# Segment maxima over neighbour windows in 640-column turned tiles, in a graph-attention kernel on one core

## The chip, the cores and the metric

The kernel runs on one core of one Trainium2 chip. A core has five engines that run side by side, each with its own stream of instructions: TensorE (PE; its weight loads are listed as PEld), VectorE (DVE), ScalarE (ACT), GpSimd (POOL) and SyncE (SP, which here only issues transfers), and 16 DMA engines that move data. The metric is the device time of one execution in microseconds (us).

## The reference

A graph has 3125 nodes with a vector x of 128 values each, and 100000 edges (src, dst, type), sorted by dst; the type is one of 5 relations. With 8 heads of 16 values, for each relation r:

```python
mask = edge_types == r
q, k, v = x_dst @ W_Q[r], x_src @ W_K[r], x_src @ W_V[r]     # per head
logits = (q * k).sum(-1) / scale + attn_bias[r]
masked = where(mask, logits, NEG)
max_v  = segment_max(masked, dst)
exp_l  = where(mask, exp(masked - max_v[dst]), 0)
attn   = exp_l / (segment_sum(exp_l, dst)[dst] + 1e-12)
out   += segment_sum(attn * v, dst)
```

Then `h = layernorm(out @ out_proj.T + b + x) * gamma + beta`, and the result is `layernorm(x + h)`. What matters below: a softmax needs the largest logit among all the edges of one node, one relation and one head, and the edges of a node lie next to each other.

## The kernel before

**Tiling.** The edges are cut into 196 groups of 512 (GE). A step k handles three groups; the last two of the 66 steps handle two. In a group, 128 edges stand on the partitions and T = 4 tiles follow each other. A lane is one (group, relation, head): 3 x 5 x 8 = 120 lanes a step, and a lane tile has the lanes on the partitions and the 512 edges of the group along its columns.

**Preamble.** x is loaded and transposed; a table of keys and values for each node and relation is written to DRAM (kv_d), the node number of each edge as key rows (key_d), the masks that mark where a new node begins (msk_d), and queries (q_d), each query in three bf16 parts so that their sum is exact enough.

**One step.** The work of an edge group goes through these functions:

- `gather` (L603): POOL issues 12 indirect transfers, each of which fetches 128 rows of kv_d into one of six K/V buffers. `gather(k+3)` stands in step k and must wait until `weigh(k-3)` has read that buffer.
- `fetch`: SP issues the keys kt (L661, 384 KB, one row spread over 128 partitions, two buffers), the query rows qw (L668, three transfers with an offset read from a register) and the masks mk (L671, three transfers, each spread over 40 lanes) of step k+3.
- `spot` (L679, DVE) compares kt with the row number into a one-hot matrix, `spread_q` (L692, PE) multiplies it with qw: 36 small products in a step give each edge its query (qe).
- `products` (L706, DVE: K times qe), `logits` (L711 sums over each head, L713 adds a hugely negative number for the relations that an edge is not in), `turn_logits` (L725, PE: four transposes to 120 lanes x 512 columns), `keep_logits` (L734, ACT: a copy).
- `scans` (L741 and L744, DVE): a running maximum forwards and one backwards along the lane, each restarted by the mask where a new node begins. The result is each edge's segment maximum within its group.
- `joins` (L760 to L763, SP): a node can reach across the end of a group. Four transfers of 120 to 320 bytes copy the last or first maximum of a lane to the neighbouring lane's partition (tile c), two of them between this step and the one before.
- `less_max`: two DVE instructions (L770) put the neighbours' maxima into the first and the last 64 columns (SEG), where the mask shows that the node goes on; a third (L774) subtracts the maximum. `exps` (L781, ACT) takes the exponential.
- `turn_exps` (L788, PE) turns the exponentials back and drops the relation axis, `weights` (L797, ACT) copies them beside the weighted values, `weigh` (L803, DVE) multiplies them with V. It is the last reader of the K/V buffer.
- `places` (L811, L814, ACT) builds a matrix that says which row of a node window each edge belongs to, `sums` (L831, L827, PE) adds the weighted values up by it, `norm` (L843 to L847, DVE) divides by the sums, `relations` (L860, PE) and `by_node` (L865, ACT) add the relations and put the nodes in place.

Two pieces of work for each block of 128 nodes come in beside this. New queries of a block are computed over three steps: `turn_q` and `turned` in the step given by a table, then `queries`, `first_part` (ACT), `remainder` (DVE), `second_part` (ACT) and `third_part` (DVE) for three relations in the next step and for two in the one after, which ends with `store_q` (L652, SP). And when all edges of a block are done, `project`, `residual` (L890, L892), `roots` and `norms` (L907) finish its nodes; x comes for both in separate transfers (`fetch_x`, tiles xq and xr, L614).

**Order.** Nothing reorders the instructions: each engine runs its own in the order of the program, and semaphores hold them until their inputs are there. The steps overlap by hand. In step k the order is: gather(k+3), queries, less_max and exps of k-2, turn_exps and weights of k-2, products, logits and turn_logits of k, keep_logits, norm of k-3, the last part of the queries and `store_q`, weigh(k-2), sums, scans(k), joins(k), `take(k)` (all of SP's loads), spot(k+2), and the block's last work. On SP this means store_q, the four joins, then kt, qw, mk and x.

Of the kernel before, what the change touches and what calls it, by code (L numbers as in the profile page):

```python
# [17 lines left out]
P = 128  # L18
N = 3125
# [36 lines left out]
MW = GE + 1 + 2 * SEG  # L56
# [67 lines left out]
def windowed_path(  # L124
# [21 lines left out]
    shut = keep("shut", [P, NST, T * G3, R], BF16)  # L146
# [25 lines left out]
    xn = load.tile([P, NT, H], F32, name="xn")  # L172
# [39 lines left out]
    dst_r = load_rows("dst_r", dst, FAR)  # L212
# [7 lines left out]
    near = load.tile([HG, 2, 2], I32, name="near")  # L220
    nc.vector.memset(near, -1)
    ends = dst[: (NGR - 1) * GE].rearrange("(g i) -> g i", i=GE)
    with nc.allow_non_contiguous_dma(reason="one element of each group"):
        nc.gpsimd.dma_start(
            lr[:, : NGR - 1],
            dst[: (NGR - 1) * GE].rearrange("(o g i) -> o g i", o=1, i=GE)[:, :, GE - 1],
        )
        nc.gpsimd.dma_start(lr[:, NGR - 1 :], dst[E - 1 : E].rearrange("(o g) -> o g", o=1))
        nc.gpsimd.dma_start(near[1:HG, 0, 0:1], ends[: HG - 1, GE - 1 : GE])
        nc.gpsimd.dma_start(near[:HR, 1, 0:1], ends[HG - 1 :, GE - 1 : GE])  # L230
        nc.gpsimd.dma_start(near[:HG, 0, 1:2], ends[1 : HG + 1, 0:1])
        nc.gpsimd.dma_start(near[: HR - 2, 1, 1:2], ends[HG + 1 :, 0:1])
        nc.gpsimd.dma_start(
            near[HR - 2 : HR - 1, 1, 1:2],
            dst[(NGR - 1) * GE : (NGR - 1) * GE + 1].rearrange("(o g) -> o g", o=1),
        )
# [3 lines left out]
    def iota(name, pattern, n, base=0, mult=0, dt=F32, pool=const):  # L240
# [21 lines left out]
    nc.vector.tensor_scalar(rsum, five, 0.0, None, op0=ALU.is_le)  # L262
    nc.vector.scalar_tensor_tensor(
        rsum, five, -float(R), rsum, op0=ALU.is_gt, op1=ALU.mult
    )
# [77 lines left out]
    def lanes():  # L343
        nc.vector.tensor_scalar(lane, lane, 0.0, None, op0=ALU.is_equal)
# [57 lines left out]
    def masks_a():  # L402
        nc.vector.memset(msk[:, :, 0:1], -BIG)
        nc.vector.memset(msk[:, :, GE : GE + 1], -BIG)
        nc.vector.tensor_tensor(
            msk[:, :, 1:GE], dst_r[:, :, 1:], dst_r[:, :, : GE - 1], op=ALU.not_equal
        )
        nc.vector.tensor_scalar_mul(msk[:, :, 1:GE], msk[:, :, 1:GE], -BIG)

    def masks_b():  # L410
        nearf = load.tile([HG, 2, 2], F32, name="nearf")
        nc.vector.tensor_copy(nearf, near)
        for s in range(2):
            for n, c in enumerate((0, GE - SEG)):
                m = GE + 1 + n * SEG
                nc.vector.tensor_scalar(
                    msk[:, s, m : m + SEG], dst_r[:, s, c : c + SEG], nearf[:, s, n : n + 1],
                    -BIG, op0=ALU.not_equal, op1=ALU.mult,
                )
# [21 lines left out]
    def put_typ(ep, s, r):  # L441
        done, g0, n = 0, s * HG, HR if s else HG
        while done < n:
# [4 lines left out]
                shut[:, k0 : k0 + m, : T * i, r].rearrange("p k (t i) -> p k t i", i=i),  # L448
# [160 lines left out]
    def fetch_x(name, b):  # L609
        n = min(P, N - b * P)  # L610
        xb = flow.tile([P, H], F32, name=name, bufs=2 if name == "xq" else 4)
        if n < P:
            nc.vector.memset(xb, 0.0)
        nc.sync.dma_start(xb[:n], x[b * P : b * P + n, :])  # L614
        live[name, b] = xb

    def turn_q(b):
        tp = ps.tile([P, P], F32, name="tp", tag="fin")
        nc.tensor.transpose(tp, live.pop(("xq", b)), ident)
# [37 lines left out]
    def fetch(k):  # L657
# [11 lines left out]
        mk = flow.tile([L3, MW], BF16, name="mk", bufs=5)  # L669
        for i, g in enumerate(gs):  # L670
            nc.sync.dma_start(  # L671
                mk[i * LANES : (i + 1) * LANES, :], msk_d[g].partition_broadcast(LANES)
            )
        live["kt", k], live["qw", k], live["mk", k] = kt, qw, mk
# [33 lines left out]
    def logits(k):  # L708
        n = T * len(groups(k))
        lg = ps.tile([P, T * G3, HEADS], F32, name="lg")[:, :n]  # L710
        nc.vector.tensor_reduce(lg, heads(live.pop(("prod", k))[:, :n]), AX.X, ALU.add)  # L711
        lx = flow.tile([P, T * G3, R, HEADS], F32, name="lx")
        nc.vector.tensor_tensor(  # L713
            lx[:, :n],
            lg[:, :, None, :].to_broadcast([P, n, R, HEADS]),
            shut[:, k, :n, :, None].to_broadcast([P, n, R, HEADS]),
            op=ALU.add,
        )
        live["lx", k] = lx

    def turn_logits(k):
        n, lx = len(groups(k)), live.pop(("lx", k))
        lt = ps.tile([L3, GE], F32, name="lt")
        for t in range(T):
            nc.tensor.transpose(  # L725
                lt[: n * LANES, t * P : (t + 1) * P],
                lx[:, t * n : (t + 1) * n].rearrange("p g r k -> p (g r k)"), ident,
            )
        live["lt", k] = lt

    def keep_logits(k):
        n = len(groups(k)) * LANES
        ls = flow.tile([L3, GE], F32, name="ls", bufs=3)
        nc.scalar.copy(ls[:n], live["lt", k][:n])  # L734
        live["ls", k] = ls

    def scans(k):
        n = len(groups(k)) * LANES
        mk, lt = live["mk", k], live.pop(("lt", k))
        m = flow.tile([L3, GE], F32, name="m", bufs=3)  # L740
        nc.vector.tensor_tensor_scan(  # L741
            lt[:n], mk[:n, :GE], lt[:n], -BIG, op0=ALU.add, op1=ALU.max
        )
        nc.vector.tensor_tensor_scan(  # L744
            m[:n, ::-1], mk[:n, GE:0:-1], lt[:n, ::-1], -BIG, op0=ALU.add, op1=ALU.max
        )
        live["m", k] = m

    def joins(k):
        n = len(groups(k)) * LANES  # L750
# [874 lines left out]
```

## Time and profile before

| what | us |
|---|---|
| median of 3 runs (lowest to highest) | 1532.03 (1531.99 to 1539.9) |
| the profiled execution | 1544.54 |
| its span, first to last instruction | 1542.7 |
| mean granted clock of TensorE | 0.694 of full speed |
| gathers: 782 instructions of POOL | 750.4 busy, 960 ns each |
| PE idle ahead of the weight loads of L692 | 333.4 |
| POOL idle ahead of the gathers | 683.6 |
| L741 scan, 120x512 | 1.22 |
| L803 weigh | 1.73 |

The profile was taken of one execution. Its page gives each engine's busy time, the chain of work that ended last, the costliest groups of instructions, and the transfers. A group's row reads: line, engine, operation, output <- inputs, count, busy time, mean ns of one, then the idle time of the engine just before these instructions and what ended most of it. A row of the waits reads: who waited <- for whom: us in total, how many times, the longest. A row of the timeline reads: start, length, engine, line, operation, and in brackets how long the engine was idle before and what released it. "issue" means that the profile shows nothing that the engine waited for; "remote" means a releaser that the trace does not hold. SPq are SP's transfers as it issues them.

### The profile page before, as it was taken

What the parts mean: (1) busy time and instruction counts of PE and PEld (TensorE: products, weight loads), DVE (VectorE), ACT (ScalarE), POOL (GpSimd) and SP (SyncE); (2) the same over time, 40 slices, a digit from 0 to 9 for tenths busy, and PEclk for the clock granted to TensorE, in tenths of its full rate; (3) what the DMA queues carried; (4) which work ended last, traced back from release to release, by engine and by line L of the source; (5) the groups of instructions that cost most, each with busy time, mean ns of one, the idle gap of its engine ahead of it and who ended that gap; (6) DMA issues with size and microseconds to landing.
All of it is one profiled execution on the core that took longest, in us unless ns stands there. A gap on an engine that the chain in (4) does not pass through costs nothing.

```text
span 1542.7 us, 18732 instructions
## 1 busy us (share of the span) xinstructions
PE 996.5 (65%) x5955; PEld 767.6 (50%) x5955; DVE 873.6 (57%) x1363; ACT 617.2 (40%) x1635; POOL 762.6 (49%) x854
## 2 busy tenths in 40 slices
PE   6930166666666656467776666767777766666875
PEld 3510154555544545356555555555555555555664
DVE  4750264656554655366665656566656665555872
ACT  2420033444434434244444444444444444444662
POOL 3067433555563563635555555555555555555300
PEclk9955567666676776676766676666666667777876
DMA  6754243444442453434444444444444444444300
GB/s 210 286 181 146 71 130 92 131 128 121 142 136 83 141 148 92 134 92 142 129 119 124 141 135 122 144 143 120 140 132 124 122 139 135 126 140 129 93 18 8
DMA packets 126821, 196.27 MB, mean 127 GB/s; under 512 B 40507, under 2 KB 86200, under 8 KB 126593
## 3 DMA queue, kind: packets, MB, share of 16 engines
q0 software_dynamic: 37856, 102.55, 22.9%
q1 hardware_dynamic: 87724, 91.13, 18.8%
q10 hardware_dynamic: 1132, 1.31, 0.3%
q8 instruction: 49, 0.80, 0.2%
q14 instruction: 60, 0.48, 0.1%
HBM read 164.43 MB, written 30.40 MB: 126 GB/s over the span
## 4 chain that ended last, share of the span: by engine, by line
PE 28%; issue 21%; another core or an unknown queue 18%; DVE 16%; ACT 7%; DMA 1%; SPq 0%; DVEq 0%; ACTq 0%
PE both L831 10%; PE qe L692 7%; DVE wv L803 3%; PE nodes L860 3%; ACT at L811 3%; PE lt L725 3%; DVE lt L741 2%; PE both L827 2%; PE ex L788 2%; DVE prod L706 2%; DVE lg L711 2%; ACT ls L781 1%; DVE m L744 1%; DVE hot L679 1%
## 5 line engine op out<-in xcount | busy, mean ns | idle before, releaser
L603 POOL DMA_INDIRECT kv<-kv_d,idx x782 | 750.4, 960 | 683.6 <-DVE wv L803 395.9
L692 PE MATMUL qe<-qw,hot 125*128 125x128 bf16 x2352 | 250.4, 262 | 311.5 <-issue 243.4
L831 PE MATMUL both<-wv,at 128*125 128x136 f32 x1568 | 370.2, 384 | 20.0 <-ACT oT L865 7.5
L692 PEld LDWEIGHTS <-hot 125*128 125x128 bf16 x2352 | 203.4, 122 | 333.4 <-issue 326.5
L831 PEld LDWEIGHTS both<-wv,at 128*125 128x125 f32 x1568 | 295.8, 263 | 96.1 <-issue 74.4
L811 ACT ACTIVATE at<-row_at,nkey 128x125 f32<-128x125 f32 x784 | 247.3, 389 | 0.1
L706 DVE TENSOR_TENSOR prod<-kv,qe 128x1536 f32<-128x1536 f32 (+1 forms) x66 | 114.2, 1731 | 55.3 <-remote 55.3
L803 DVE TENSOR_TENSOR wv<-kv,ex 128x1536 f32<-128x1536 f32 (+1 forms) x66 | 114.2, 1730 | 36.4 <-ACT wv L797 36.4
L741 DVE TENSOR_TENSOR_SCAN lt<-mk,lt 120x512 f32<-120x512 bf16 (+1 forms) x66 | 80.6, 1222 | 87.8 <-ACT ls L734 87.8
L814 ACT ACTIVATE at<-at 128x500 f32<-128x500 f32 x196 | 121.6, 620 | 6.2
L725 PE MATMUL lt<-ident,lx 128*120 128x128 f32 (+1 forms) x264 | 73.4, 397 | 77.7 <-issue 70.4
L734 ACT COPY ls<-lt 120x512 f32<-120x512 f32 (+1 forms) x66 | 38.8, 587 | 206.5 <-PE lt L725 116.6
L711 DVE TENSOR_REDUCE lg<-prod 128x96 f32<-128x1536 f32 (+1 forms) x66 | 115.1, 1745 | 2.3
L860 PE MATMUL nodes<-rsum,o 125*128 125x25 f32 x392 | 87.7, 359 | 41.8 <-issue 30.1
L860 PEld LDWEIGHTS nodes<-rsum,o 125*128 125x128 f32 x392 | 85.5, 307 | 48.0 <-issue 33.6
L788 PE MATMUL ex<-gather_heads,ls 120*128 120x24 f32 (+1 forms) x528 | 71.9, 275 | 52.7 <-ACT ls L781 30.1
L788 PEld LDWEIGHTS ex<-gather_heads,ls 120*128 120x128 f32 (+1 forms) x528 | 68.8, 200 | 72.7 <-ACT ls L781 40.7
L639 DVE TENSOR_TENSOR prq<-prq,q 128x384 f32<-128x384 f32 (+1 forms) x42 | 20.9, 497 | 146.6 <-ACT q L635 120.8
L827 PE MATMUL both<-wv,over 128*5 128x136 f32 x390 | 97.1, 340 | 0.0
L725 PEld LDWEIGHTS lt<-ident,lx 128*120 128x120 f32 (+1 forms) x264 | 45.0, 196 | 104.0 <-issue 93.6
L797 ACT COPY wv<-ex 128x96 f32<-128x96 f32 (+1 forms) x66 | 15.8, 239 | 191.2 <-remote 182.2
L635 ACT CAST q<-prq 128x384 bf16<-128x384 f32 (+1 forms) x42 | 17.7, 422 | 184.2 <-remote 172.9
(157 smaller groups left out, 940.7 us busy)
## 6 DMA issues: line engine op xcount, KB each, us to landing
kt<-key_d SPq DMA_DIRECT2D x64, 384.0 KB
qw<-q_d SPq DMA_DIRECT2D x196, 96.0 KB
kv_d<-kvs SPq DMA_DIRECT2D x24, 640.0 KB
kv<-kv_d,idx POOLq DMA_INDIRECT x782
q_d<-q SPq DMA_DIRECT2D x25, 480.0 KB
mk<-msk_d SPq DMA_DIRECT2D x196, 50.1 KB
c<-m SPq DMA_DIRECT2D x134, 0.2 KB
c<-m SPq DMA_DIRECT2D x128, 0.3 KB
```

The lines of the kernel that those rows point to most:

```text
L603: nc.gpsimd.indirect_dma_start(out=kv[:, t * n + i, :], out_offset=None, in_=kv_d[:, :], in_offset=bass.IndirectOffsetOnAxis(ap=idx[:, t, ...
L692: nc.tensor.matmul(qe[:, t * n + i, :], hot[:, i, t * P : (t + 1) * P], qw[:WR, i, s, :], start=(s == 0), stop=(s == 2),)
L706: nc.vector.tensor_tensor(prod[:, :n], kv[:, :n, :H], qe[:, :n], op=ALU.mult)
L711: nc.vector.tensor_reduce(lg, heads(live.pop(("prod", k))[:, :n]), AX.X, ALU.add)
L725: nc.tensor.transpose(lt[: n * LANES, t * P : (t + 1) * P], lx[:, t * n : (t + 1) * n].rearrange("p g r k -> p (g r k)"), ident,)
L788: nc.tensor.matmul(ex[:, t * n : (t + 1) * n], ls[: n * LANES, t * P : (t + 1) * P], gather_heads[: n * LANES, :n], start=True, stop=True,)
L803: nc.vector.tensor_tensor(heads(wv[:, :n, :H]), heads(kv[:, :n, H:]), ex[:, :, :, None].to_broadcast([P, n, HEADS, HD]), op=ALU.mult,)
L811: nc.scalar.activation(at[:, t, :], row_at[:, :WR], AF.Abs, bias=nkey[:, t, g : g + 1], scale=1.0)
L814: nc.scalar.activation(at, at, AF.Relu, bias=1.0, scale=-1.0)
L827: nc.tensor.matmul(pp[:R], over[:, g, :], live["wv", last][:, t * len(groups(last)) + j, :], start=False, stop=False,)
L831: nc.tensor.matmul(pp[:WR], at[:, t, :], wv[:, t * n + i, :], start=(t == 0), stop=(t == T - 1))
L860: nc.tensor.matmul(nodes[:, i], o5[:, i], rsum[:WR], start=True, stop=True)
```

## The change

1. **Windows instead of joins.** A lane now sees 64 logits of the group before and 64 of the group behind, so the scans run over 640 columns and find each maximum without its neighbours' help. The logits tile gets room for one more group per tile of edges. `near` (DVE, 64 x 40) writes the first 64 edges of this step's first group into the tile of the step before; `pass_on` (ACT, 64 x 40) copies the last 64 edges of the step into the next step's tile. Turning takes two more transposes of 64 edges: one in `turn_logits`, one in `turn_next`. The scans work in place in PSUM, over two banks. `joins`, the tiles m and c, and the two L770 instructions are gone. The masks are 641 wide and come from rows of dst that reach into the neighbours, which replaces five small loads by POOL and four small mask operations in the preamble.
2. **Masks** come in one transfer a step (`fetch_masks(k+1)`, three buffers) instead of three in `fetch(k+3)` (five buffers).
3. **x stays on chip** (xn); `fetch_x` and its 46 transfers are gone.
4. **Order.** `scans`, `less_max` and `exps` of k-1 now stand late in step k; step k begins with `turn_exps` and `weights` of k-2 and the turning of k-1's logits. `logits(k)` comes after `weigh(k-2)`, `spot(k+2)` and the last third of `spread_q` before the scans. On SP a step now has `store_q` (where there is one), kt, qw, mk and the output.
5. `shut` is laid out with the relation ahead of the group; two instructions on `rsum` move within the preamble.

The number of SP's transfers in the steps falls from 12.5 to about 5.7 a step; PE's transposes rise from 264 to 396 in all.

The core of the diff:

```diff
-MW = GE + 1 + 2 * SEG
+WIDE = GE + 2 * SEG
+MW = WIDE + 1
...
+    def fetch_masks(k):
+        n = len(groups(k))
+        live["mk", k] = mk = flow.tile([L3, MW], BF16, name="mk", bufs=3)
+        rows = msk_d[G0[k] : G0[k] + n]
+        nc.sync.dma_start(
+            mk[: n * LANES, :],
+            bass.AP(tensor=rows.tensor, offset=rows.offset, ap=[[MW, n], [0, LANES], [1, MW]]),
+        )
...
+    def near(a, k, p, i):
+        q = slice(p, p + SEG)
+        nc.vector.tensor_tensor(
+            a,
+            live["lg", k][q, i : i + 1, :].to_broadcast([SEG, R, HEADS]),
+            shut[q, k, :, i : i + 1].to_broadcast([SEG, R, HEADS]),
+            op=ALU.add,
+        )
...
+    def pass_on(k):
+        n = len(groups(k))
+        if k + 1 < NST:
+            nc.scalar.copy(
+                lanes_of(k + 1)[P - SEG :, (T - 1) * (G3 + 1)],
+                live["lx", k][P - SEG :, (T - 1) * (G3 + 1) + n],
+            )
...
     def turn_logits(k):
-        n, lx = len(groups(k)), live.pop(("lx", k))
-        lt = ps.tile([L3, GE], F32, name="lt")
+        live["lt", k] = ps.tile([L3, 4 * GE // 2], F32, name="lt")
         for t in range(T):
...
+            turned_lanes(k, 2 * SEG + t * P, 0, P, t * (G3 + 1) + 1)
+        turned_lanes(k, SEG, P - SEG, SEG, (T - 1) * (G3 + 1))
+
+    def turn_next(k):
+        turned_lanes(k, 2 * SEG + GE, 0, SEG, 2)
...
     def scans(k):
...
+        mk, lt = live.pop(("mk", k)), live["lt", k][:n, SEG : SEG + WIDE]
         nc.vector.tensor_tensor_scan(
-            lt[:n], mk[:n, :GE], lt[:n], -BIG, op0=ALU.add, op1=ALU.max
+            lt, mk[:n, :WIDE], lt, -BIG, op0=ALU.add, op1=ALU.max
         )
...
-    def joins(k):
...
-                nc.sync.dma_start(q[e - LANES : e, 1:2], m[:LANES, 0:1])
-                nc.sync.dma_start(c[:LANES, 0:1], p[e - LANES : e, GE - 1 : GE])
-            nc.sync.dma_start(c[LANES:n, 0:1], m[: n - LANES, GE - 1 : GE])
-            nc.sync.dma_start(c[: n - LANES, 1:2], m[LANES:n, 0:1])
...
-        for s, e in enumerate((0, GE - SEG)):
-            w = GE + 1 + s * SEG
-            nc.vector.scalar_tensor_tensor(
-                m[:n, e : e + SEG], mk[:n, w : w + SEG], c[:n, s : s + 1], m[:n, e : e + SEG],
-                op0=ALU.add, op1=ALU.max,
-            )
```

and of the order in a step:

```diff
         if q is not None:
             queries(q, c0, c1)
-        shares(k - 2)
-        place_next()
+        if old:
+            exped(k - 2)
+        if new:
+            lanes_turned(k - 1)
         if q is not None:
             first_part(q, c0)
-        if old:
-            turn_exps(k - 2)
-            weights(k - 2)
         products(k)
         spread_q(k + 1, [0, 1])
-        logits(k)
-        turn_logits(k)
         if q is not None:
             remainder(q, c0)
             second_part(q, c0)
-        keep_logits(k)
-        spread_q(k + 1, [2])
+        place_next()
         if groups(k - 3):
             norm(k - 3)
         if q is not None:
             third_part(q, c0)
             if c0:
                 store_q(q)
-        place_next()
         if groups(k - 3):
             relations(k - 3)
             by_node(k - 3)
         if old:
             weigh(k - 2)
         sum_next()
+        logits(k)
+        pass_on(k)
         if q0 is not None:
             turn_q(q0)
             turned(q0)
         place_next()
-        scans(k)
-        joins(k)
-        take(k)
+        if new:
+            turn_next(k - 1)
+        spread_q(k + 1, [2])
+        if k + 2 < NST:
+            spot(k + 2)
         sum_next()
         if done is not None:
             project(done)
-        if k + 2 < NST:
-            spot(k + 2)
+        if new:
+            shares(k - 1)
+        take(k)
+        if groups(k - 1):
+            places(G0[k - 1])
         sum_next()
```

Here `shares` is scans, less_max and exps, `exped` is turn_exps and weights, and `lanes_turned` is turn_logits and keep_logits.

## The prediction

> **What bounds the kernel now.** I read, in this order, the page's busy times and chain, the waits, the timeline of two steps in the middle, and the busy time in stretches of those steps.
>
> ```profile
> PE 996.5 (65%) x5955; PEld 767.6 (50%) x5955; DVE 873.6 (57%) x1363; ACT 617.2 (40%) x1635; POOL 762.6 (49%) x854
> PE 28%; issue 21%; another core or an unknown queue 18%; DVE 16%; ACT 7%; DMA 1%; SPq 0%; DVEq 0%; ACTq 0%
> ```
> ```profile
> POOL kv L603 <- DVE wv L803: 395.9, 56, 36.9
> PEld L692 <- issue: 326.5, 222, 53.0
> ACT wv L797 <- remote: 182.2, 35, 8.1
> ACT q L635 <- remote: 172.9, 30, 8.2
> ```
> No engine is full. POOL waits 395.9 us for the weighing (L803), which frees a K/V buffer; PE's weight loads of L692 wait 326.5 us for nothing visible ("issue"), and ACT 182.2 and 172.9 us for a signal that comes late ("remote"). The timeline of one step shows these together:
> ```profile
> 800.07 0.94 POOL L603 DMA_INDIRECT kv<-kv_d,idx  x1 [6.76 <-DVE wv L803]
> ...
> 802.22 0.82 SPq L760 DMA_DIRECT2D c<-m  x1
> ...
> 805.12 0.59 SPq L661 DMA_DIRECT2D kt<-key_d  x1
> ...
> 814.90 0.37 PE L725 MATMUL lt<-ident,lx 128*120 128x128 f32 x1 [1.84 <-issue]
> ...
> 816.31 0.37 PE L725 MATMUL lt<-ident,lx 128*120 128x128 f32 x1 [1.03 <-issue]
> ...
> 817.09 0.24 ACT L797 COPY wv<-ex 128x96 f32<-128x96 f32 x1 [6.05 <-remote]
> 817.97 1.75 DVE L803 TENSOR_TENSOR wv<-kv,ex 128x1536 f32<-128x1536 f32 x1
> 819.99 0.94 POOL L603 DMA_INDIRECT kv<-kv_d,idx  x1 [5.17 <-DVE wv L803]
> ```
> A weighing ends at T0 = 799.8. POOL issues 12 gathers from 800.07 (0.95 and a 0.30 gap each, 15.0 us), to T0+15.3. Some us after SP starts the keys' load (kt, 384 KB, T0+5.3), PE slows: transposes that take 0.37 us come 1.41 apart (with its weight load each, 0.70 us an instruction); I call this the dribble. About 2 us after the last gather PE and ACT run again (T0+17.3), the exps are copied (0.24), L803 runs (1.75): T0+19.8. The stretches give the size:
> ```profile
> 830.80:837.00 6.20, 1.29 (x8) 0.43 (x6) 1.17 (x2) 0.00 (x0) 3.21 (x4) 0.53 0.47 142
> 837.00:841.30 4.30, 4.16 (x26) 3.77 (x26) 3.65 (x7) 3.46 (x10) 0.00 (x0) 0.50 0.00 2
> ```
> In the next step's dribble (first row; columns are length, PE, PEld, DVE, ACT, POOL, clock, DMA share, GB/s) PE is busy 1.29 us with the DMA engines 47% busy; when POOL and the DMA fall still it is busy 4.16 of 4.30. Summed over the span, such stretches are some 446 us. The end of a step is thus set by: last gather, 2 us, then what PE, ACT and DVE could not finish before.
>
> From one weighing to the next it takes 19.4 us in a step without queries (A), 21.6 with the first part of a query block (B, its ACT and DVE chain follows the dribble), 19.9 with the second part (C, which ends in the store of q). Steps 3 to 57 are about 14 cycles ABC (60.9) and 7 cycles BC (41.5). Four times an interval is only 14.3, ahead of the dribble; POOL then never pauses, and the next takes 34.1, 37.3, 34.8 and 36.7. Each pair costs 9.2 to 10.1 us more than its normal one, **39 us** in all. The last steps, without gathers, take 13.1.
>
> **The change, part by part.**
> - *Joins and their SP wait* (L760 to L763: 0.82+0.76+0.56+0.59 = 2.7 us of SP a step). SP no longer waits for the scans, so kt is asked for when its buffer is free, after the spot of the step (T0+3.3, from L803's end: sums of L711 1.75, near 0.2, L713 0.66, spot 0.6). DVE loses two L770 (2 x 0.28) and their waits (12.7 and 62.1 us in all, beside the dribble, costed at 0).
> - *Masks and x.* mk: three issues to one, the same bytes; xq/xr: 46 loads of 64 KB gone. They stand on SP behind kt; SPq has 0% of the chain: 0.
> - *Added.* Scans 512 to 640 columns: 1.22 to 1.53, twice, +0.61; near (64x40) 0.2 by L843's 0.18, between 0.06 by column from L713 and 0.31 by L845; so DVE +0.3 a step. PE: two transposes of 64 columns, 0.13 to 0.27 each (four of 128 take 1.06). ACT: pass_on, 0.2 (L797: 0.24). In A and B all of it lies beside the gathers; if that cover were gone, 0.3 x 66 = 20 us. In the preamble POOL loses five issues (0.55 each) and DVE four small mask operations: -2, between 0 and -4.
> - *Order.* Scans, less_max and exps go into the step before; in a step only turned exps (1.07), the copy and L803 remain ahead of the weighing. SP is now held in C alone, at the store of q, until its third part, 1.8 us before L803's end. So no keys are loaded between the weighings B to C, and no dribble comes: I add the rows. Scans start T0+3.3, 2 x 1.53, L774 0.75, L781 0.63, L788 1.07, L797 0.24, keep 0.59, then q's parts 0.43, 0.42, 0.38, norm 1.05 and the last part 0.41, L803 1.75: 14.1, with hops of some 0.15 **15.8** (14.3 where before had no dribble). In A the end of the gathers still decides: 19.4. In B keep_logits (0.59) now stands ahead of the first part on ACT: 22.1.
> - *What is late next.* After C the held kt goes out as POOL begins its next block, and a second kt at T0+3.3: PE has about 3 us of work ahead of the slow issue (as at 805 to 810), and dribbles from T0+3 to T0+17.3, 14 us for 6 to 7. Behind the gathers then stand the sums of two groups (2 x 2.0), L788 1.07 less about 1 dribbled, 0.24 and 1.75: 17.3+6.1 = 23.4, say **23.5** for A; for B 2.5 more, **26**. Nothing in a normal step shows this. The lower end is 19.4/22.1 (early dribble costs nothing), the upper one the double intervals, 34.8/37.0. I take the sum of rows, as these upper rows hold joins, a residual's wait and the old order's scans behind the gathers.
>
> Sum: ABC 23.5+22.1+15.8 = 61.4 (+0.5, x14 = +7); BC 26+15.8 = 41.8 (+0.3, x7 = +2); the four doubles -39, as POOL's pauseless passage after C is now in the 23.5; preamble -2. Together **-32** on the profiled execution's 1544.5 us (span 1542.7 and 1.8 around it): 1512.5. That execution lies 12.5 above the median 1532.0, which I subtract: **1500**.
>
> One rule speaks against any gain. The Trainium skill, "DMA: Bandwidth & Descriptors", section "Issuing engines are not separate DMA queues", says that all engines' transfers interleave on the same 16 DMA engines and that where they are issued only saves the issuing sequencer's time. By it, copies that go save SP's issue alone, which has 0% of the chain: the time would be that of the second rival. The trace agrees in the chain's 0%, and does not show that issue time is all, since PE stalls with the DMA engines half idle.
>
> **The rivals.**
> 1. *Slower: the keys after the store of q.* Their load meets the whole next block. For it: the 37.3 of before, with 17.6 us from PE's return (477.5) to the weighing's end (495.1). Against: joins (2.6) and a residual's wait (3.8) in it go. 17.3+17.6-6.4 = 28.5: with 28 for A and 30 for B, ABC is 65.9 (+5.0, x14 = +70), BC 45.8 (+4.3, x7 = +30), less 41: +59, **1591**. It decides from 32/21 = 1.5 us above my value, 25.0 for A.
> 2. *Same: gathers and 2 us still end every step, and doubles stay.* The kt load, not the small copies, begins the dribble; new short intervals make new doubles. For it: A's 19.4 holds nothing that the change removes. Against: SP's hold goes from two of three intervals. **1532**. This is also the rival that the change does not do what it says: SP's wait only moves to the store of q.
> 3. *Much faster: an early dribble costs nothing.* The new order leaves PE little behind the gathers: 19.4+22.1+15 = 56.5 (-4.4, x14 = -62), 37.1 (-4.4, x7 = -31), -41: **1398**. Beyond it, if the dribble hung on the number of SP's transfers and went altogether, POOL alone would set 15.3 a step: 56 x (20.4-15.3) = -286, -41: about 1205. Against: in the preamble (107.9) kt starts it with no joins before.
>
> **How the numbers follow.** Forecast 0.40 (own range 1470 to 1530), rival 1 0.36, rival 2 0.10, rival 3 0.14 (0.04 of it the last). 0.5% (7.7 us) is about what a measurement can tell from no change. Faster: 0.38 of the forecast and 0.14, 0.52; same: 0.10 and 0.02, 0.12; slower 0.36. The range, 1395 to 1615, holds the forecast, rivals 1 and 2 and most of 3; left out are the 1205, and doubles' intervals in full after each C (about 1735), with the edges some 0.15.
>
> **What would show it.** SP waits no more on DVE's L770 line but at the store of q; intervals of 15 to 16 ahead of C's weighing without PE "issue" waits, and 23 to 26 behind; POOL's wait for the weighing near 0 there; no interval over 30. It is wrong if C's interval is dribbled too, if the dribble begins without kt, or if PE's issue waits are gone.

## The result, and the profile after

The changed kernel takes 1597.05 us (median of 4 runs, 1586.5 to 1604.74) beside 1535.97 for the kernel before: ratio 1.0369, 95% interval 1.0263 to 1.0474. It is slower; the forecast was 1500. The profiled execution has a span of 1602.9 us, 60.2 more than the one shown of before.

What everything below needs: in some of the later comparisons the kernel before itself took 1145 to 1147 us, and no profile taken there has a single wait for a "remote" signal or a dribble. So each experiment is read against the kernel before beside it, and "with the dribble" (the expectations call it the slow stretch) means that this took 1532 to 1538 us.

The page of the changed kernel (busy times, chain) and its waits:

```profile
PE 1026.0 (64%) x6087; PEld 776.9 (48%) x6087; DVE 887.8 (55%) x1288; ACT 637.9 (40%) x1700; POOL 765.3 (48%) x850
another core or an unknown queue 26%; DVE 26%; PE 22%; ACT 13%; issue 9%; DMA 2%; POOL 1%; DVEq 0%; ACTq 0%
```
```profile
POOL kv L603 <- DVE wv L817: 452.6, 60, 30.7
DVE prq L631 <- ACT q L627: 320.0, 42, 9.4
ACT wv L811 <- remote: 286.5, 48, 8.4
PEld L688 <- issue: 270.5, 215, 57.0
...
DVE h L906 <- remote: 140.4, 16, 10.1
```

Two more waits of the first profile, of the kernel before:

```profile
DVE prq L639 <- ACT q L635: 120.8, 20, 7.0
DVE h L892 <- PE pj L873: 57.7, 20, 4.2
```

PE's issue waits ahead of the query products fell from 326.5 to 270.5 us, but ACT's wait for a "remote" signal ahead of the weights rose from 182.2 to 286.5, DVE's for the first part of the queries from 120.8 to 320.0, and the residual (L892 before, L906 after), which waited 57.7 us for PE's projection, now waits 140.4 for a "remote" signal. POOL waits 452.6 us for the weighing instead of 395.9. SP's own waits moved as forecast, from the joins to the store of q:

```profile
SPq L644 <- DVE q L640: 649.1, 21, 34.7
SPq L653 <- DVE hot L675: 238.8, 20, 15.7
```

The time from the end of one weighing to the next, by kind of step, for weighings 3 to 57 (means in us; CA and CB are A and B behind a step that stores q; "before" is the profile b_same below, which has one double interval at the start where the first profile had four; "rest" is the other intervals between weighings; what follows the last weighing, some 22.5 us, is the same in both):

| | B (14) | C (20) | CA (14) | CB (6) | rest | to the first weighing |
|---|---|---|---|---|---|---|
| before, b_same, span 1513.0 | 21.4 | 20.0 | 19.7 | 21.5 | 174.9 in all | 212.2 |
| forecast | 22.1 | 15.8 | 23.5 | 26 | | |
| after, span 1602.9 | 22.3 | 21.7 | 21.4 | 26.1 | 176.8 in all | 201.4 |
| difference in all | +13.8 | +34.3 | +23.5 | +27.3 | +1.9 | -10.8 |

These add up to the 90 us between the two spans. The medians lie 61 us apart; b_same is one execution, 18 us faster than the median of the kernel before beside it. The step that decides is C. Its timeline in the changed kernel, from the first gather of the block to the weighing:

```profile
440.89 0.95 POOL L603 DMA_INDIRECT kv<-kv_d,idx  x1 [7.33 <-DVE wv L817]
...
448.61 1.07 PE L802 MATMUL ex<-gather_heads,ls 120*128 120x24 f32 x8
...
454.89 0.95 POOL L603 DMA_INDIRECT kv<-kv_d,idx  x1 [0.30 <-issue]
456.52 0.24 ACT L811 COPY wv<-ex 128x96 f32<-128x96 f32 x1 [6.15 <-remote]
457.97 0.59 ACT L771 COPY ls<-lt 120x512 f32<-120x512 f32 x1 [1.20 <-remote]
458.45 0.38 ACT L627 CAST q<-prq 128x256 bf16<-128x256 f32 x1
...
460.23 0.41 DVE L640 TENSOR_TENSOR q<-prq,q 128x256 bf16<-128x256 f32 x1
460.56 1.75 DVE L817 TENSOR_TENSOR wv<-kv,ex 128x1536 f32<-128x1536 f32 x1
460.67 0.34 SPq L644 DMA_DIRECT2D q_d<-q  x1
461.06 0.43 SPq L653 DMA_DIRECT2D kt<-key_d  x1
```

No keys are loaded in this interval: SP, whose last transfer before it was issued at 429.92, is held until 460.67, as forecast. The dribble is there all the same, as this stretch of the block shows (columns as in the prediction: length, PE, PEld, DVE, ACT, POOL, clock, DMA share, GB/s):

```profile
451.00:455.84 4.84, 1.46 (x15) 0.64 (x12) 0.00 (x0) 0.00 (x0) 3.79 (x4) 0.91 0.37 108
```

PE is busy 1.46 of 4.84 us although its granted clock is 0.91 and the DMA engines are 37% busy, so neither a lowered clock nor full DMA engines make the dribble here. PE ends the turned exponentials at 449.68, 8.8 us after the block's first gather, but ACT goes on only at 456.52, after the last gather; the trace's record of the semaphore has PE's update at 456.50, so it is the signal that is late and not ACT. Behind it ACT still has keep_logits and the first part of the queries to do, DVE the remainder and the third part. In the kernel before the first part stood ahead of the weights on ACT.

### The profile page after: what moved, and what is told of

It reads as the page before. It is cut to its first block, busy times and chain, and to the rows that moved or that the text cites. A ratio compares the mean times of both kernels' runs of the same rounds, so it can differ in the third digit from the quotient of the medians.

```text
span 1602.9 us, 18517 instructions
## 1 busy us (share of the span) xinstructions
PE 1026.0 (64%) x6087; PEld 776.9 (48%) x6087; DVE 887.8 (55%) x1288; ACT 637.9 (40%) x1700; POOL 765.3 (48%) x850
## 4 chain that ended last, share of the span: by engine, by line
another core or an unknown queue 26%; DVE 26%; PE 22%; ACT 13%; issue 9%; DMA 2%; POOL 1%; DVEq 0%; ACTq 0%
PE both L845 7%; DVE lt L780 4%; DVE lt L777 4%; ACT at L825 4%; PE pr L366 3%; DVE wv L817 3%; PE nodes L874 3%; PE qe L688 3%; DVE lg L722 3%; DVE prod L702 2%; ACT at L828 2%; DMA floor<-in_L_gnn_attn_bias 2%; PE both L841 2%; ACT ls L795 1%
## 5 line engine op out<-in xcount | busy, mean ns | idle before, releaser
L603 POOL DMA_INDIRECT kv<-kv_d,idx x782 | 755.2, 966 | 740.3 <-DVE wv L817 452.6
L688 PE MATMUL qe<-qw,hot 125*128 125x128 bf16 x2352 | 263.3, 277 | 323.9 <-issue 224.4
L688 PEld LDWEIGHTS <-hot 125*128 125x128 bf16 x2352 | 204.0, 127 | 363.9 <-issue 270.5
L845 PE MATMUL both<-wv,at 128*125 128x136 f32 x1568 | 366.3, 375 | 17.6 <-ACT oT L879 10.8
L845 PEld LDWEIGHTS both<-wv,at 128*125 128x125 f32 x1568 | 283.5, 251 | 90.0 <-issue 63.8
L874 PE MATMUL nodes<-rsum,o 125*128 125x25 f32 x392 | 91.9, 378 | 142.9 <-DVE q L640 136.1
L811 ACT COPY wv<-ex 128x96 f32<-128x96 f32 (+1 forms) x66 | 15.6, 236 | 311.6 <-remote 286.5
L777 DVE TENSOR_TENSOR_SCAN lt<-mk,lt 120x640 f32<-120x640 bf16 (+1 forms) x66 | 98.6, 1493 | 34.5 <-issue 19.7
L780 DVE TENSOR_TENSOR_SCAN lt<-mk,lt 120x640 f32<-120x640 bf16 (+1 forms) x66 | 98.7, 1495 | 2.3
L906 DVE TENSOR_TENSOR h<-pj,xn 128x128 f32<-128x128 f32 (+1 forms) x25 | 7.3, 291 | 158.1 <-remote 140.4
L795 ACT ACTIVATE ls<-ls 120x512 f32<-120x512 f32 (+1 forms) x66 | 41.6, 630 | 127.0 <-DVE ls L787 49.2
L752 PE MATMUL lt<-ident,lx 128*120 128x128 f32 (+2 forms) x396 | 84.0, 309 | 4.8 <-DVE lx L711 2.0
L802 PEld LDWEIGHTS ex<-gather_heads,ls 120*128 120x128 f32 (+1 forms) x528 | 75.3, 213 | 20.4 <-issue 10.3
L743 ACT COPY lx<-lx 64x40 f32<-64x40 f32 x65 | 14.4, 222 | 162.5 <-DVE lx L728 153.1
```

What stands on the lines that cost most here:

```text
L603: nc.gpsimd.indirect_dma_start(out=kv[:, t * n + i, :], out_offset=None, in_=kv_d[:, :], in_offset=bass.IndirectOffsetOnAxis(ap=idx[:, t, ...
L688: nc.tensor.matmul(qe[:, t * n + i, :], hot[:, i, t * P : (t + 1) * P], qw[:WR, i, s, :], start=(s == 0), stop=(s == 2),)
L777: nc.vector.tensor_tensor_scan(lt, mk[:n, :WIDE], lt, -BIG, op0=ALU.add, op1=ALU.max)
L780: nc.vector.tensor_tensor_scan(lt[:, ::-1], mk[:n, WIDE:0:-1], lt[:, ::-1], -BIG, op0=ALU.add, op1=ALU.max)
L845: nc.tensor.matmul(pp[:WR], at[:, t, :], wv[:, t * n + i, :], start=(t == 0), stop=(t == T - 1))
L874: nc.tensor.matmul(nodes[:, i], o5[:, i], rsum[:WR], start=True, stop=True)
```

## The experiments

Theory K is the prediction's: the keys' transfer beside the gathers starts the dribble. Theory G: the stream of gathers alone does. Theory T: the loss is work put behind the dribble by the new order. Theory W: the wider windows themselves cost the time. Theory S makes T exact: a signal that PE sends later than some 7 us into a block of gathers reaches ACT and DVE only behind the block. Code cuts are shortened where they have "...".

**1. Without the keys** (b_no_keys, b_no_keys2).

```diff
-        kt = flow.tile([P, G3, GE], BF16, name="kt", bufs=2)
-        nc.sync.dma_start(kt[...], key_d[...])
+        if k < 2:
+            live["key", k] = flow.tile([P, G3, GE], BF16, name="kt", bufs=2)
+            nc.sync.dma_start(live["key", k][...], key_d[...])
+        kt = live["key", k % 2]
```

> The kernel before, with the keys' transfer (kt, 384 KB a step) left out from the third step on, so that the one-hot matrices are built from old keys; the gathers and all other work stay. Theory K (the prediction's): the keys' transfer beside the gathers starts the stretch in which PE, ACT and SP issue one instruction per 0.70 us. Then the stretch is gone, PE's issue waits ahead of L692 fall from 326 us to under 60, a step comes near POOL's 15.3 us, and the time falls to 1220 to 1320 us. Theory G: the stream of gathers alone starts it, some 10 us after its first gather, and it lasts until 2 us after the last. Then the intervals between two weighings stay at 19 to 22 us, the stretch stays at 6 to 7 us a step, and the time is 1490 to 1540 us. What speaks for G so far: in the changed kernel no keys are loaded ahead of the weighing of a step that stores q, and the interval is still 21.7 us.

Measured: 1145.68 us, but the kernel before took 1147.49 beside it (ratio 0.9987, 0.9975 to 1.0), so it told nothing between the theories. Again, with the dribble:

> The kernel before without the keys' transfer from the third step on (the one-hot matrices are built from old keys), again, in case the stretch of slow issue is there this time. With the stretch: theory K (the keys start it) 1220 to 1320 us, theory G (the gathers alone) 1490 to 1540 us. Without it: 1140 to 1150 us by either, which tells nothing between them.

Measured: 1562.52 us in its one profiled execution (the kernel before 1532.62), above the 1490 to 1540 of theory G; it has six double intervals. Its waits:

```profile
POOL kv L603 <- DVE wv L805: 414.9, 54, 35.2
PEld L694 <- issue: 315.3, 208, 55.0
...
ACT q L635 <- remote: 173.5, 30, 8.2
```

These are the waits of before (395.9, 326.5, 172.9), and the intervals, outside the double ones, are 21.5 in B and 19.9 in C. Theory K falls: in the steps, keys are not needed for the dribble. Theory G is not shown by this alone, since SP's other loads stayed; it has for it the interval C above, in which the gathers are the only transfers issued. Against it as stated stands the preamble: there gathers ran from 83.8 us on, and SP's first slow transfers (three of qw, 9.8 us, 2.0 in b_paced2) come at 110.6, behind the first keys at 107.9. What starts the dribble there stays open.

**2. Slower gathers** (b_paced, b_split, b_paced2). One POOL memset of 128x256 (0.34 us) behind each gather, shown here; in b_split six of them behind the sixth gather of a block.

```diff
                     in_offset=bass.IndirectOffsetOnAxis(ap=idx[:, t, g : g + 1], axis=0),
                 )
+                nc.gpsimd.memset(idle, 0.0)
```

> The kernel before, with one POOL memset of 128x256 (some 0.3 us) behind each of the 782 gathers, so that a block of 12 takes about 18.5 us instead of 15.0 and its transfers come at four fifths of the rate. Theory G1: the stretch of slow issue is a backlog of the gathers' transfers, which builds up as POOL issues faster than they drain. Then it comes later or not at all, PE's issue waits fall to under half of 326 us, the interval is near POOL's own 18.8 us or a little over, and the time is 1450 to 1530 us. Theory G2: any stream of gathers does it whatever the rate, until 2 us after the last one. Then each interval grows by the 3.5 us that the block grows by, to 23 and more, the slow stretch to about 10 us a step, and the time to 1720 to 1770 us. Theory K (the keys) gives the same as G2.

> The kernel before, with six POOL memsets of 128x256 (some 1.8 us) behind the sixth gather of each block, so that the stream pauses once. Theory G1 (a backlog): it drains in the pause, the stretch of slow issue shrinks from 6 to 7 us a step to 2 or less, and the interval is set by the block, 15.0 + 1.8 and the 4 us behind it or less: 17 to 21 us, the time 1400 to 1560 us with PE's issue waits under half of 326 us. Theory G2 (any stream, or a count of gathers): the stretch begins as before, some 10 us after the first gather, and lasts 1.8 us longer; intervals 21 to 23.5 us, the time 1620 to 1670 us.

Measured, both without the dribble: 1290.79 (ratio 1.1247, 1.1206 to 1.1288) and 1278.36 (1.1139, 1.1109 to 1.1168). Neither theory's case. In all 47 blocks in the middle of both traces POOL went on to the next block without a pause, so POOL's own instructions set the step there (17.5 us a block in b_paced). With the dribble:

> The kernel before with one POOL memset of 128x256 behind each gather, again; where there was no slow stretch it took 1291 us, POOL's own 1.6 us a gather and more. With the stretch: theory G1 (a backlog of the gathers' transfers, which a lower rate avoids) 1340 to 1480 us, with PE's issue waits ahead of L692's line under 160 us and late signals gone; theory G2 (any stream of gathers) 1700 to 1800 us, with the waits of before and a longer stretch. Without it: 1285 to 1295 us.

Measured: 1528.54 us in one execution (before 1538.38), although a block of gathers takes 17.2 us for 14.9 (the 12 memsets, 4.1 us, lie in part in the gaps between gathers). PE's issue waits fell as G1 had it, the late signals did not go:

```profile
POOL kv L606 <- DVE wv L807: 204.6, 28, 10.6
...
ACT ls L738 <- remote: 182.1, 23, 10.6
...
PEld L696 <- issue: 82.1, 102, 5.6
```

So the rate matters (G2's 1700 to 1800 is refuted), but 0.87 of it doesn't end the dribble: neither G1 nor G2 as stated. What it gains lies in the preamble: the first weighing ends at 150.1 us for 211.7 in the first profile and 151.1 without the dribble (b_mask_x). In the steps it gains nothing: POOL went on without a pause behind 23 of 47 blocks and waited the longer behind the others, and from one block to the next it is 21.0 us on average, as in the first profile.

**3. The changed and the kernel before again** (a_same, b_same, a_same2).

> The changed kernel once more, beside the kernel before in the same place. In the first experiments the kernel before took 1147 us, its steps 14 to 16 us, and no stretch of slow issue was in any of their profiles. Theory T (the loss is work placed behind the stretch of slow issue): where the kernel before takes near 1147 us, there is no stretch, and the changed kernel is not slower: ratio 0.98 to 1.01; where it takes near 1532 us, the ratio is 1.03 to 1.05 again. Theory W (the wider windows cost it by their own work, +0.3 us of DVE and 0.5 of PE a step): the ratio is 1.02 to 1.05 in both.

> The kernel before once more, for its profile. If its time is near 1147 us: PE's issue waits ahead of L692 under 100 us for 326, POOL idle ahead of the gathers under 350 us for 684, intervals between two weighings of 14 to 17 us, which POOL's 15.0 us a block sets. If its time is near 1532 us: the profile as first shown.

Measured, with the dribble: 1598.47 and before 1532.62 (ratio 1.0469, 1.0387 to 1.0551), as both T and W have it there, so it doesn't decide between them. b_same was 1514.82 us in one execution; its waits are those of the first profile (L692 issue 326.4), its intervals those of the table.

> The changed kernel itself, beside the others. With the slow stretch 1590 to 1605 us, ratio 1.03 to 1.05. Without it (the kernel before near 1147 us): theory T (the loss is work behind the stretch) a ratio of 0.98 to 1.01, theory W (the windows' own work) 1.02 to 1.05.

Measured: 1637.47, before 1538.38: ratio 1.064 (1.0582 to 1.0697), above what was expected. CA is 23.0 here and 21.1 in a_same; which of the two it takes varies. The changed kernel itself was never measured without the dribble.

**4. keep_logits back behind the second part** (a_keep_late, a_keep_late2).

```diff
-    def lanes_turned(k):
+    def lanes_turned(k, keep_too=True):
         turn_logits(k)
-        keep_logits(k)
+        if keep_too:
+            keep_logits(k)
...
         if new:
-            lanes_turned(k - 1)
+            lanes_turned(k - 1, False)
...
             remainder(q, c0)
             second_part(q, c0)
+        if new:
+            keep_logits(k - 1)
```

> The changed kernel with keep_logits(k-1) put back behind the second part of the queries on ACT, as in the kernel before; all else as changed. Theory T: the loss is what stands behind the slow stretch in a step with queries, where ACT does keep_logits (0.59 us) and only then the first part. Then the interval ahead of a step that stores q falls from 21.7 to 19.9 to 21.2 us, that of a step with the first part from 22.3 to 21.5 to 21.9, and the time by 20 to 45 us, to 1552 to 1577. The rival W: the wider windows themselves cost it (scans of 640 columns, two more transposes, the copies): then the intervals and the time stay within 8 us of 1597.

Measured, without the dribble: 1135.24 us for 1147.49: ratio 0.9908 (0.9875 to 0.994). The numbers of the expectation don't apply; but this kernel has all the windows of the change, and it is faster there. That speaks against W.

> The changed kernel with keep_logits(k-1) back behind the second part of the queries, again, in case the slow stretch is there this time (the kernel before near 1532 us). Then theory T expects the interval ahead of a step that stores q at 19.9 to 20.6 us for 21.7 and that with the first part at 21.5 to 21.8 for 22.3, which is 20 x 1.5 + 14 x 0.7 = 40 us less: 1545 to 1570 us. Theory W (the windows' own work) expects 1590 to 1600 us. Without the stretch (the kernel before near 1147 us), 1130 to 1140 us again.

Measured, with the dribble: 1609.2 us, where the changed kernel takes 1637.47: -28. The 1545 to 1570 of T was missed: the gain is less than the 40 it expected, and the changed kernel itself took 40 us more here than the 1597 it started from. C went from 22.0 to 21.4, B from 22.6 to 22.1, CB from 26.4 to 25.0. The direction is T's, the size in C is a third of what T said (0.54 for 1.5): this copy is not the main part.

**5. project ahead** (a_project_first).

```diff
             turn_q(q0)
             turned(q0)
+        if done is not None:
+            project(done)
         place_next()
...
         sum_next()
-        if done is not None:
-            project(done)
         if new:
             shares(k - 1)
```

> The changed kernel with project(done), two products of PE, moved ahead of the last lane transposes and of two groups of sums, so that its end is signalled some 3 us after the first gather of a block instead of 7. In the changed kernel's trace DVE waits 140 us in all for this signal, up to 10.2 us at a time although PE had ended the work. Theory S (a signal that PE sends later than some 7 us into a block of gathers reaches the other engines only behind the block): with the stretch, the intervals behind a step that stores q fall from 23.0 and 26.9 to 20.2 and 22.5, DVE's wait at that line to under 40 us, and the time by 25 to 60 us, to 1535 to 1570. The rival (the wait is PE's own work or PSUM's buffer): the wait stays above 100 us and the time within 10 us of 1597. Without the stretch: 1125 to 1150 us, the wait small anyway.

What it mends, in the timeline of the changed kernel's first profile (a CB interval, block from 462.58 to 477.57):

```profile
469.69 0.48 PE L887 MATMUL pj<-lift,ones 1*128 1x128 f32 x2
...
480.13 0.29 DVE L906 TENSOR_TENSOR h<-pj,xn 128x128 f32<-128x128 f32 x1 [10.14 <-remote]
480.48 1.65 PE L622 MATMUL prq<-wq,xTq 128*128 128x384 f32 x2 [8.67 <-DVE h L906]
```

PE ends the projection at 470.17, DVE hears of it at 480.1 (the semaphore's update is recorded at 480.11) and stands still until then, and PE in turn waits for DVE to free the buffer. Measured: 1581.07, above the 1535 to 1570 expected, but 56.4 less than a_same2 beside it, within the 25 to 60. CA went from 22.96 to 20.55 and CB from 26.40 to 22.73: 14 x 2.41 + 6 x 3.67 = 56. The wait at L906 is, of 188.8 us for a remote signal in a_same2, now:

```profile
DVE h L906 <- PE pj L887: 2.9, 2, 2.2
```

PE ends the same work 3.0 to 5.0 us into the block instead of 6.5 to 8.5, and DVE, busy until then, takes it up some 4.4 us later without a wait. So the late signal is the cause, and not PE's work or the buffer. The "only behind the block" of S is too strong, however: of the 21 projections of the first profile that end 6.5 to 8.5 us into a full block, DVE takes up 13 behind the block's last gather, 6 after a wait of 3.0 to 7.0 us up to 4.8 us before it, and 2 at once. What decides between them the runs do not show. CA goes with it: in that profile it is 20.1 us where the wait was 4.2, and 23.0 where it was 10.1.

**6. The first part back ahead of the weights** (a_first_first, which also has the edit of experiment 4; and with the edit of 5 besides a_three, a_three2, a_three3).

```diff
             queries(q, c0, c1)
+            first_part(q, c0)
         if old:
             exped(k - 2)
...
-        if q is not None:
-            first_part(q, c0)
         products(k)
```

> The changed kernel with keep_logits behind the second part (as in a_keep_late) and the first part of the queries put back ahead of the weights on ACT, as in the kernel before: there the first part and the remainder are over when the slow stretch comes, in the changed order the first part stands behind the weights, whose release from PE comes only after the block of gathers. Theory T (order): with the stretch, the interval ahead of a step that stores q goes to 19.9 to 20.3 us (21.4 in a_keep_late2, 22.0 in the changed kernel), that with the first part to 21.5 to 21.8, and the time to 1560 to 1585 us where the changed kernel takes 1637. Theory W (wider windows): 21.4 and 22.0 stay. Where there is no stretch: 1125 to 1145 us.

> The changed kernel with all three places of the order mended: keep_logits behind the second part, the first part ahead of the weights, project(done) ahead of the last lane transposes; windows, masks in one transfer and x on chip as changed. Theory T: the whole loss is in these three places, so the intervals are near those of before (C 20, B 21.6, behind C 19.5 to 20.5 and 21.5 to 22.7), and the time is 1500 to 1535 us where the kernel before takes 1532: ratio 0.975 to 1.00, the rest a gain of 10 us from the shorter preamble and from no double blocks. Theory W: 1560 us and more. Where there is no stretch: 1120 to 1140 us for 1147.

Measured, without the dribble: 1134.11 (ratio 0.9904, 0.9875 to 0.9933) and 1134.78 (0.9915, 0.9889 to 0.9941). Once more:

> The changed kernel with the three places of the order mended, again, as it has been measured only where there is no slow stretch (1135 us for 1146). With the stretch (the kernel before near 1532 us) theory T (the loss is work whose PE signal comes behind the block of gathers) expects intervals of 19.9 to 20.3 us ahead of the step that stores q (21.7 to 22.0 in the changed kernel), 21.5 to 21.8 with the first part (22.3 to 22.6), 19.4 to 20.5 and 21.5 to 22.7 behind the store (20 to 23.2 and 25 to 27), and a ratio to the kernel before of 0.975 to 1.00. If something else of the change costs time there, intervals C or B stay within 0.3 us of the changed kernel's and the ratio is above 1.01. Without the stretch: ratio 0.99 again.

Measured, without it again: 1133.44, ratio 0.9895 (0.9869 to 0.9922). With the dribble:

> The changed kernel with the three places of the order mended, once more. With the stretch of slow issue (the kernel before near 1532 us): theory T (the loss is work whose PE signal comes behind the block of gathers) 1500 to 1550 us, intervals C 19.9 to 20.3 (21.7 to 22.0 in the changed kernel) and B 21.5 to 21.8 (22.3 to 22.6); theory W (the wider windows' own work) 1570 us and more. Without the stretch: 1130 to 1138 us, ratio 0.99.

Measured: 1530.12 us for 1536.88: ratio 0.9955 (0.9939 to 0.9971). C is 20.3, B 21.8, CA 20.5, CB 21.9, and DVE's and ACT's waits at the three places shrink against the first profile after:

```profile
DVE prq L631 <- ACT q L627: 214.8, 34, 8.6
ACT wv L811 <- remote: 154.3, 34, 8.1
...
DVE h L906 <- PE pj L887: 2.9, 2, 2.2
```

Against a_same2, in another comparison whose kernel before took 1538.38: C 1.7 x 20, B 0.76 x 14, CA 2.46 x 14, CB 4.47 x 6 make 106 us, and the times differ by 107. Against the 1597 of the first result it is 67. Either way the ratio to the kernel before falls from 1.037, 1.047 and 1.064, in three comparisons, to 0.9955 with all the windows kept: the three places of the order account for the loss, and W falls as its cause. That the windows cost a little is not excluded: the intervals are 0.3 to 0.8 us above those of b_same, 26 us in all, though b_same was a fast execution. What the first part alone brings with the dribble was not measured; 107 - 28 - 56 leaves an estimate of 23 us. Against the kernel before this version is 0.4% faster with the dribble and 1% without, and nothing of that lies in the steps: with the dribble its first weighing ends at 199.6 us for 212.2 in b_same, without it at 136.4 (a_three) for 151.1 (b_mask_x, experiment 7), which is more than the whole gain both times.

**7. Masks and x alone** (b_mask_x): the kernel before with one transfer for the masks of a step, and x kept in SBUF (xr and xq read from xn).

> The kernel before with two parts of the change alone: masks in one transfer a step, and x kept on chip, without its 46 transfers. Both theories: no change beyond 0.5%, ratio 0.995 to 1.005, since SPq has 0% of the chain and no engine waits for x or the masks; below 0.99 it would be a gain of its own.

Measured, without the dribble: 0.9993 (0.9977 to 1.0009), no change, as expected. With the dribble it was not tried. The profile shows what the kernel then hangs on: the row of the gathers has no wait for the weighing at all, and a block of gathers starts every 15.3 us.

```profile
L603 POOL DMA_INDIRECT kv<-kv_d,idx x782 | 759.7, 971 | 304.2 <-issue 226.4 <-DVE rem L547 66.3 <-DVE m L771 4.0
```

**8. Half rows** (b_half, b_half2): `out=kv[..., :H]` from kv_d seen as rows of 128 values.

> The kernel before with gathers of half a row (512 B an edge instead of 1 KB, the same 782 instructions; the keys come from wrong rows and the values are ones). Theory G-bytes (the stretch is a backlog of the bytes gathered): with the stretch on this kernel before, it goes, the signals from PE come in time, and the time falls to POOL's bound, 1130 to 1250 us. Theory G-count (it hangs on the number of gathered rows or of POOL's instructions): the stretch stays, 1480 to 1540 us. Where the kernel before takes near 1147 us: 1130 to 1150, which tells nothing.

Measured, without the dribble: 1141.77 (ratio 0.9963, 0.9942 to 0.9984).

> The kernel before with gathers of half a row (512 B an edge, the same 782 instructions; the keys come from wrong rows and the values are ones), again, as it has run only where there is no stretch. With the stretch (the kernel before near 1535 us): theory G-bytes (a backlog of the gathered bytes) 1130 to 1300 us and PE's issue waits ahead of L692's line under 150 us; theory G-count (the number of rows or of POOL's instructions) 1480 to 1540 us and waits near 320. Without it 1130 to 1150, which tells nothing.

Measured, again without it: 1142.96 (0.9976, 0.9957 to 0.9994). Whether the dribble hangs on the bytes of the gathers or on their number stays open.

## Why the prediction was wrong, point by point

- *What bounds the kernel.* Right as to the place (last gather, 2 us, then what is left); wrong as to the cause. The keys had followed the first gather by some 5 us in the steps that were read, and they were taken for the trigger of the dribble. b_no_keys2 shows it without keys.
- *Order: "So no keys are loaded between the weighings B to C, and no dribble comes".* This is the step that failed. The first half came true (SP is held at L644 for 649.1 us), the second not. 15.8 was forecast for C and 21.7 measured; over 20 intervals that is 118 us, more than the 97 between forecast and result. The rows were right up to the turned exponentials, ready at 449.68 and within 1 us of their sum; the signal of it came 6.8 us late, and the rest of the chain stood behind the block. A dribble in C's interval is what the prediction itself named first as a sign of being wrong.
- *B.* 22.1 forecast, 22.3 measured: keep_logits ahead of the first part, as said, and the first part behind the weights, which was overlooked.
- *What is late next.* 23.5 and 26 forecast behind C, 21.4 and 26.1 measured (21.1 to 23.0 and 25.3 to 26.4 in the others). That the size is near is chance, since the reason was different: not two groups of sums left over by an early dribble, but DVE standing in the residual for a PE signal (a_project_first gives back 56 us).
- *Rival 1* said 1591, near the 1597 measured, but by 28 and 30 behind C and 15.8 ahead of it. Neither came; its time was right by chance.
- *Rival 2 and the skill's rule.* The Trainium skill, "DMA: Bandwidth & Descriptors", section "Issuing engines are not separate DMA queues", says that starting transfers on several engines at once saves only the sequencer's time to start them. That transfers which go altogether save no more than SP's issue time was the prediction's own step from there. Without the dribble b_mask_x fits it: it changes nothing (0.9993). The joins alone were not taken out.
- *The doubles.* Intervals over 30 are gone in the changed kernel, as forecast. But b_same has only one of them (34.0 at its start) at 1514.82 us, and b_no_keys2 has six: their number varies from one execution to the next, and the -39 belonged to the one that was shown. The forecast took it off twice in part: three doubles fewer, at some 9.7 us each, are 29 of the 29.7 us between the spans of the two executions, and the 12.5 us by which the first lay above the median were subtracted as well.
- *Preamble.* -2 forecast; the first weighing ends 10.8 us earlier. Which part of it gives that was not tried.
- *Windows.* 1.53 forecast for a scan of 640 columns, 1.49 measured; near 0.19, pass_on 0.22. They lay beside the gathers, as said; that they made the steps shorter, no run shows.

## What to carry to other kernels

Two things that follow each other in every step of a trace can't be told apart by it: before a forecast rests on one as the trigger, look for a place where only one of them happens, or count it a rival. When work is moved in a hand-written order, ask of every signal not only when its engine is done but in which stretch it is sent, and what stands behind the waiting instruction; a copy or a residual that waits in order holds all that follows. What differs between two comparisons of the same kernel (here 385 us in the kernel before) can be larger than any change: measure the two kernels side by side, each time.

## What the runs showed of the hardware

With the dribble, a signal of PE sent 7.6 and 8.8 us after a block's first gather arrived 10 us (L887 to L906) and 6.8 us (L802 to L811) after PE's work had ended, in both cases once the gathers were over; other signals at L906 were late by less, and two not at all (experiment 5). Where PE ended 3.0 to 5.0 us into the block (a_project_first), DVE did not wait for its signal. POOL's and DVE's own instructions kept their lengths: 0.96 us for a gather and 1.73 for the weighing in the kernel before, 0.97 and 1.73 without the dribble (b_mask_x). Nor were the gathers' transfers slower: their packets took 22.9% of 1542.7 us on the 16 DMA engines with the dribble and 35.7% of 1143.8 without, 353 and 408 us. The mean granted clock of the profiled executions was 0.68 to 0.71 with the dribble and 0.78 to 0.82 without; in the dribble of interval C above it was 0.91, so the lower mean does not explain the dribble.

The kernel before took 1145 to 1147 us without the dribble instead of 1532 to 1538. What makes it come and go between comparisons, none of the runs shows. It is not the chip alone: on chip 10, as the results name it, the kernel before took 1147 us in one comparison and 1537 in a later one.
